# The feed-forward value product as three products of rounded high and low parts, with a new plan of phases

## The chip, the cores and the metric

The kernel runs on one core of a Trainium2 chip. The metric is the device time of one launch in microseconds (us). The times shown are medians over several runs of the same program; one further execution was profiled.

## The reference

The input is `x` of shape (8, 1024, 256) in 32-bit floats: 8 sequences of 1024 tokens with 256 channels. Three layers are added to it in turn.

```python
x = x + 0.5 * ffn(layernorm(x), W_r, W_k, W_v, mu_r, mu_k)
x = x + attention(layernorm(x), qkv_w, qkv_b, out_w, out_b, gate_w, gate_b, pos_bias, scale_embed, if_gain)
x = x + 0.5 * ffn(layernorm(x), W_r, W_k, W_v, mu_r, mu_k)

def ffn(x, W_r, W_k, W_v, mu_r, mu_k):
    x_prev = x shifted by one token, with zeros in front
    xr = mu_r * x + (1 - mu_r) * x_prev
    xk = mu_k * x + (1 - mu_k) * x_prev
    r = sigmoid(xr @ W_r.T)
    k = xk @ W_k.T
    return r * (square(relu(k)) @ W_v.T)
```

The attention has 16 heads of 16 channels. Each token looks at 40 fixed distances behind it (0 to 32, and 48, 64, 96, 128, 192, 256, 384), with a logit that is scaled by a learned vector for each distance, a softmax over the 40, and a sigmoid gate ahead of the output projection. All three weight matrices of the feed-forward layer are 256 x 256, and both feed-forward layers use the same ones. The change is in the last product, `square(relu(k)) @ W_v.T`.

## The kernel before

The 8192 tokens are cut into 32 chunks of 256. For each chunk the program has three generators: `ffn(c, "a")` (the first feed-forward layer), `project(c)` (the projections of the attention) and `ffn(c, "b")` (the second feed-forward layer). The attention has `far` and `local`, which compute scores by blocks and write them to HBM skewed, and `attend(tt)` for each tile of 128 tokens, which reads them back, adds the bias, takes the softmax and multiplies with the values.

Each `yield` ends a phase. The order of all work is written out by hand: the table `PLAN` gives every phase of a generator a place in units of chunks, `WARP` shifts the places of the first four and the last ten chunks, and at the end of `macaron` all phases are sorted by place and run in that order. So each engine has a fixed queue of instructions, served in order. A phase that is moved in `PLAN` moves its instructions on every engine and its transfers in the queues of SP and ACT.

One feed-forward layer on one chunk goes so:

- `normed` (L206 to L226): statistics on DVE, eight small instructions on POOL, the scaling on ACT (L224), and four transposes on PE (L226), which leave channels on partitions.
- the mixing with the token before: four instructions on ACT (L241), four on DVE (L246) into the tile `xm`; `xk` and `xr` are its halves.
- the key product with `wk`: four 32-bit products of 128 x 128 by 256 columns, then the relu on ACT (L263) back into `xk`.
- the gate product with `wr`, four more, and the square of `xk` on ACT (L269, in place), then the tanh (L271).
- the value product with `wv`, four more, with `xk` as the stationary side: `mm(p[:, i], xk[:, h, i * 128 : i * 128 + 128], wv[:, h], h == 0, h == 1)`.
- the gating on DVE (L278) and the addition to the token's row on POOL (L280).

The attention's projections in `project` are already made of high and low parts in 16-bit floats: `wa_hi`, `wa_lo` for the weights, `xh` and `xl` for the data, and three products (high by high, high by low, low by high) in place of each one. ACT rounds `xh` (L291), and DVE computes the rest `xl` (L292). In the profile a 32-bit product appears as two records, a 16-bit one as one.

PSUM has three banks for these products (`bank`, the tag `psf`). `xm`, and so `xk`, has one buffer for each of the two layers.

Of the kernel before, what the change touches and what calls it, by code (L numbers as in the profile page):

```python
# [7 lines left out]

F32 = mybir.dt.float32
F16 = mybir.dt.float16  # L10
I32 = mybir.dt.int32
AF = mybir.ActivationFunctionType
# [30 lines left out]


PLAN = {
    "setup": (94.301, 95.430, 96.861),
    "f1": (-6.891, -5.181, -4.113, -3.628, -3.556, -3.503, -3.223, -3.134, -3.030, -2.933, -2.814, -2.771),
    "p": (-2.636, -2.595, -2.382, -2.366, -2.209, -2.155, -2.084, -1.868, -1.644, -1.528, -1.432),
    "f2": (1.626, 1.748, 1.930, 2.004, 2.060, 2.208, 2.297, 2.414, 2.553, 2.580, 2.713, 4.437),
    "far": (  # L50
        (-0.987, -0.918),
        (-0.874, -0.608),
        (-0.990, -0.939),
        (-0.777, -0.772),
        (-0.751, -0.627),
        (-0.528, -0.523),
    ),
    "loc": (
        (-1.515, -1.348),
        (-0.848, -0.610),  # L60
        (-1.298, -1.048),
        (-1.496, -1.489),
    ),
    "att": (
        (-0.277, -0.025, -0.020, 0.011, 0.092, 0.296, 0.358, 0.413, 0.416, 0.471, 0.743, 0.779, 0.784, 0.838, 0.892, 0.971, 1.094, 13.222),
        (-0.404, 0.000, 0.016, 0.041, 0.111, 0.194, 0.295, 0.315, 0.427, 0.447, 0.621, 0.660, 0.673, 0.723, 0.824, 0.884, 0.938, 1.093),
    ),
}
WARP = {
    ("att", 0): 0.012, ("att", 1): 0.014, ("att", 2): 0.002, ("att", 3): -0.006, ("att", 22): 0.010, ("att", 23): 0.002, ("att", 24): -0.008, ("att", 25): 0.032, ("att", 26): 0.048, ("att", 27): 0.036, ("att", 28): 0.026, ("att", 29): -0.049, ("att", 30): -0.064, ("att", 31): -0.076,  # L70
    ("f1", 0): -1.203, ("f1", 1): -0.910, ("f1", 2): -0.739, ("f1", 3): 0.153, ("f1", 22): 0.006, ("f1", 23): 0.025, ("f1", 24): -0.009, ("f1", 25): -0.004, ("f1", 26): 0.009, ("f1", 27): 0.026, ("f1", 28): 0.017, ("f1", 29): 0.027, ("f1", 30): 0.045, ("f1", 31): 0.053,
    ("f2", 0): 0.006, ("f2", 1): 0.006, ("f2", 2): -0.013, ("f2", 3): 0.001, ("f2", 22): 0.006, ("f2", 23): -0.003, ("f2", 24): 0.043, ("f2", 25): 0.041, ("f2", 26): 0.025, ("f2", 27): 0.477, ("f2", 28): 0.422, ("f2", 29): 0.543, ("f2", 30): 0.373, ("f2", 31): 0.119,
    ("far", 0): -0.275, ("far", 2): -0.001, ("far", 22): 0.004, ("far", 24): 0.035, ("far", 26): 0.044, ("far", 28): 0.047, ("far", 30): -0.024,
    ("loc", 0): -0.699, ("loc", 1): -0.010, ("loc", 2): 0.023, ("loc", 3): 0.047, ("loc", 22): 0.037, ("loc", 23): 0.007, ("loc", 24): 0.043, ("loc", 25): 0.074, ("loc", 26): 0.045, ("loc", 27): 0.056, ("loc", 28): 0.007, ("loc", 29): 0.037, ("loc", 30): 0.014, ("loc", 31): 0.120,
    ("p", 0): -0.906, ("p", 1): -0.868, ("p", 2): -0.096, ("p", 3): 0.024, ("p", 22): -0.017, ("p", 23): -0.005, ("p", 24): 0.014, ("p", 25): 0.005, ("p", 26): -0.008, ("p", 27): -0.040, ("p", 28): 0.034, ("p", 29): 0.045, ("p", 30): 0.006, ("p", 31): -0.018,
}


# [5 lines left out]
def macaron(ctx: ExitStack, tc: tile.TileContext, x, wffn, watt, wo, cols, rows, pbias, se, mask, out):  # L84
    nc = tc.nc
# [3 lines left out]

    ident = const.tile([128, 128], F32, name="ident")  # L90
    make_identity(nc, ident)
    w_f = const.tile([128, 3, 2, 256], F32, name="w_f")
    wr, wk, wv = w_f[:, 0], w_f[:, 1], w_f[:, 2]
    col = const.tile([128, 14], F32, name="col")
    mu_r, mu_k, b_q, b_k, b_g, gain, slot = (col[:, 2 * i : 2 * i + 2] for i in range(7))
    wot = const.tile([128, 2, 256], F32, name="wot")
# [25 lines left out]
    pga = pool("pga", PGA)  # L122
    lazy = {}

    def setup():
        with tc.tile_pool(name="setup", bufs=1) as sp:
            nc.sync.dma_start(w_f, wffn.rearrange("w (c p) d -> p w c d", p=128))
            wst = sp.tile([128, 4, 2, 256], F32, name="wst")
            nc.sync.dma_start(wst, watt.rearrange("w (c p) d -> p w c d", p=128))
            nc.sync.dma_start(row, rows.unsqueeze(0).to_broadcast([128, 2, 256]))  # L130
            zero = sp.tile([128, 4 * 512], F32, name="zero")
            nc.gpsimd.memset(zero, 0.0)
            nc.sync.dma_start(bias[:, 3].rearrange("p u e -> p (u e)"), pbias.to_broadcast([128, NO * 16]))
            msk = sp.tile([128, 3, NO], F32, name="msk")
            nc.sync.dma_start(msk, mask.rearrange("t p u -> p t u"))
            nc.sync.dma_start(wot, wo.rearrange("(c p) d -> p c d", p=128))
            se_f = sp.tile([128, NO], F32, name="se_f")
            nc.sync.dma_start(se_f, se.unsqueeze(0).to_broadcast([8, 16, NO]))
            yield
            nc.gpsimd.tensor_scalar(w_f[:, 2], w_f[:, 2], 0.25, 0.0, ALU.mult, ALU.add)  # L140
            for t in vw:
                nc.gpsimd.memset(t, 0.0)
            for t in ks:
                nc.gpsimd.memset(t[:, 0:LW], 0.0)
            for i in range(2):
                nc.sync.dma_start(v_d[i][0 : VPAD * VROW].rearrange("(p w) -> p w", p=VPAD), zero[:VPAD, :VROW])
            for sf in sf_d:
                nc.sync.dma_start(sf[0:PADF].rearrange("(p w) -> p w", p=16), zero[:16, : PADF // 16])
                for c0, c1, w in ((0, 5, 384), (5, 10, 384), (10, 15, 384), (15, 16, 368)):
                    o = PADF + c0 * ROW + ROW - 384  # L150
                    nc.sync.dma_start(flat(sf, o, (SF_T, 32), (ROW, c1 - c0), (1, w)), zero[:32, : (c1 - c0) * w])
            nc.sync.dma_start(flat(pd_d, NL * 16, (4 * SKEW, 128), (SKEW, 4), (1, SKEW - NL * 16)), zero[:, : 4 * 512])
            nc.vector.tensor_scalar(wst[:, 0], wst[:, 0], 0.25 * WS, None, ALU.mult)
            nc.vector.tensor_scalar(wst[:, 1:4], wst[:, 1:4], WS, None, ALU.mult)
            nc.scalar.copy(wa_hi, wst)
            nc.vector.tensor_tensor(wa_lo, wst, wa_hi, ALU.subtract)
            nc.vector.tensor_scalar(b_q, b_q, 0.25 * WS, None, ALU.mult)
            nc.vector.tensor_scalar(b_k, b_k, WS, None, ALU.mult)
            nc.vector.tensor_scalar(bv, bv, WS, None, ALU.mult)
            nc.vector.tensor_scalar(b_g, b_g, 0.5, None, ALU.mult)  # L160
            yield
            for t in range(3):
                nc.gpsimd.tensor_tensor(
                    bias[:, t], bias[:, 3], msk[:, t].unsqueeze(2).to_broadcast([128, NO, 16]), ALU.add
                )
            for c in range(2):
                nc.vector.tensor_scalar(wot[:, c], wot[:, c], gain[:, c : c + 1], 0.5 / WS, ALU.mult, ALU.mult)
            nc.vector.tensor_scalar(se_f, se_f, 4.0 / WS, None, ALU.mult)

            nc.vector.tensor_reduce(  # L170
                own.rearrange("p (h q) -> p h q", h=2),
                ident.rearrange("p (q h d) -> p h q d", q=4, h=2),
                AX.X,
                ALU.add,
            )
            nc.vector.tensor_reduce(
                kown.rearrange("p (h q) -> p h q", h=2),
                own.rearrange("p (h r q) -> p h q r", h=2, r=2),
                AX.X,
                ALU.add,  # L180
            )
            nc.vector.tensor_tensor(
                seb.rearrange("p u h q -> p u (h q)"),
                se_f.unsqueeze(2).to_broadcast([128, NO, 4]),
                kown.unsqueeze(1).to_broadcast([128, NO, 4]),
                ALU.mult,
            )
        lazy["pat"] = pool("pat", 2)
        lazy["pv1"] = pool("pv1", 2)
        yield  # L190
# [3 lines left out]
    def mm(o, l, r, start, stop):  # L194
        nc.tensor.matmul(o, l, r, start=start, stop=stop)  # L195
# [34 lines left out]
    def ffn(c, s):  # L230
# [35 lines left out]
        for i in range(2):  # L266
            for h in range(2):
                mm(p[:, i], xr[:, h, i * 128 : i * 128 + 128], wr[:, h], h == 0, h == 1)
        nc.scalar.activation(xk, xk, AF.Square)  # L269
        yield  # L270
        nc.scalar.activation(xr, p, AF.Tanh, scale=0.5)  # L271
        yield
        p = bank([128, 2, 256], "p")
        for i in range(2):
            for h in range(2):
                mm(p[:, i], xk[:, h, i * 128 : i * 128 + 128], wv[:, h], h == 0, h == 1)
        yield
        nc.vector.scalar_tensor_tensor(xr, xr, 1.0, p, ALU.add, ALU.mult)  # L278
        yield
# [290 lines left out]
    add = lambda kind, place, gen, times: steps.extend(  # L570
        (move(kind, place) + t, kind, j, gen) for j, t in enumerate(times)
    )
    add("0", -100, setup(), PLAN["setup"])
    for c in range(NCH):
        add("f1", c, ffn(c, "a"), PLAN["f1"])
        add("p", c, project(c), PLAN["p"])
# [73 lines left out]
```

## Time and profile before

| | |
|---|---|
| median of 3 runs | 1022.88 us (1022.44 to 1028.41) |
| the profiled execution's own time | 1026.83 us |
| its span | 1024.8 us |
| PE busy | 951.4 us (93%) |
| PEld busy (weight loads, beside PE) | 781.3 us (76%) |
| DVE busy | 831.9 us (81%) |
| POOL busy | 695.5 us (68%) |
| ACT busy | 610.4 us (60%) |
| DMA | 208.75 MB, 204 GB/s |

PE is TensorE, DVE is VectorE, ACT is ScalarE, POOL is GpSimd, and SP is the engine that issues most transfers. A share of the span averages over a start, a long middle and an end. In the start and the end few chunks are under way, and the engines wait for each other; in the middle the phases of many chunks overlap. The span is the profiled execution's, on the one core.

### The profile page before, as it was taken

What the parts mean: (1) busy time and instruction counts of PE and PEld (TensorE: products, weight loads), DVE (VectorE), ACT (ScalarE), POOL (GpSimd) and SP (SyncE); (2) the same over time, 40 slices, a digit from 0 to 9 for tenths busy, and PEclk for the clock granted to TensorE, in tenths of its full rate; (3) what the DMA queues carried; (4) which work ended last, traced back from release to release, by engine and by line L of the source; (5) the groups of instructions that cost most, each with busy time, mean ns of one, the idle gap of its engine ahead of it and who ended that gap; (6) DMA issues with size and microseconds to landing.
All of it is one profiled execution on the core that took longest, in us unless ns stands there. A gap on an engine that the chain in (4) does not pass through costs nothing.

```text
span 1024.8 us, 36078 instructions
## 1 busy us (share of the span) xinstructions
PE 951.4 (93%) x14592; PEld 781.3 (76%) x14592; DVE 831.9 (81%) x1670; ACT 610.4 (60%) x1218; POOL 695.5 (68%) x1240
## 2 busy tenths in 40 slices
PE   3888899999999999999999999999999999976775
PEld 2666688888888888888888888888888888854554
DVE  4446889988999789888999789988999789866761
ACT  3454666676666766676666766676666766543332
POOL 5434778767877688667787678767886778543641
PEclk9899999999999999999999999999999999988888
DMA  8257777768777776777877777688776777757530
GB/s 241 62 157 204 221 227 200 222 200 249 214 219 216 215 237 198 214 228 218 236 207 225 220 237 211 196 236 244 222 212 210 205 227 216 211 161 234 166 110 21
DMA packets 204365, 208.75 MB, mean 204 GB/s; under 512 B 77288, under 2 KB 162472, under 8 KB 204200
## 3 DMA queue, kind: packets, MB, share of 16 engines
q1 hardware_dynamic: 194984, 189.16, 64.8%
q10 hardware_dynamic: 9216, 17.31, 4.6%
q8 instruction: 114, 1.87, 0.8%
q14 instruction: 51, 0.42, 0.1%
HBM read 110.26 MB, written 96.14 MB: 201 GB/s over the span
## 4 chain that ended last, share of the span: by engine, by line
PE 81%; DMA 4%; POOL 4%; DVE 4%; issue 3%; ACT 2%; SPq 1%; ACTq 0%; POOLq 0%; DVEq 0%
PE p L195 55%; PE pv L195 6%; PE tra L195 5%; PE tra L514 5%; PE tr L226 5%; PE gp L195 4%; PE tra L547 1%; DMA lg<-sl 1%; ACT xn L224 1%; POOL y L213 1%; POOL x L280 1%; DMA sf<-sf 1%; DVE prod L505 1%; DMA pd<-pd 1%; DVE st L207 1%
## 5 line engine op out<-in xcount | busy, mean ns | idle before, releaser
L195 PE MATMUL p<-w_f,xm 128*128 128x256 f32 x1024 | 251.3, 389 | 0.0
L195 PEld LDWEIGHTS p<-w_f,xm 128*128 128x128 f32 x1024 | 187.5, 192 | 42.2 <-issue 12.7
L461 POOL TENSOR_TENSOR lg<-lg,bias 128x640 f32<-128x640 f32 x64 | 99.0, 1547 | 85.8 <-DVE lg L458 74.6
L195 PE MATMUL p<-xm,w_f 128*128 128x256 f32 x512 | 128.6, 396 | 8.4 <-DVE xm L248 5.2
L224 ACT ACTIVATE xn<-x,nb,y 128x256 f32<-128x256 f32 x192 | 104.9, 599 | 32.4 <-POOL nb L219 16.4
L241 ACT ACTIVATE xm<-tr,col 128x256 f32<-128x256 f32 x256 | 100.4, 475 | 39.8 <-PE tr L226 33.9
L195 PE MATMUL p<-kst,qst 64*32 64x256 f32 (+1 forms) x4096 | 123.6, 362 | 0.5 <-DVE kst L317 0.3
L246 DVE SCALAR_TENSOR_TENSOR xm<-tr,rest,xm 128x255 f32<-128x255 f32 x256 | 105.5, 474 | 21.2 <-ACT xm L241 19.9
L195 PEld LDWEIGHTS p<-xm,w_f 128*128 128x128 f32 x512 | 96.5, 198 | 25.6 <-issue 10.4
L508 POOL TENSOR_TENSOR far<-prod 128x272 f32<-128x272 f32 x64 | 49.0, 765 | 93.3 <-DVE prod L505 86.2
L280 POOL TENSOR_TENSOR x<-x,xm 128x512 f32<-128x512 f32 x64 | 81.9, 1279 | 39.9 <-DVE xm L278 39.9
L195 PE MATMUL p<-xh,wa_hi 128*128 128x256 f16 x384 | 105.1, 274 | 0.0
L195 PE MATMUL p<-xh,wa_lo 128*128 128x256 f16 x384 | 104.9, 273 | 0.0
L195 PE MATMUL p<-xl,wa_hi 128*128 128x256 f16 x384 | 104.9, 273 | 0.0
L482 POOL TENSOR_TENSOR prod<-vn,lg 128x272 f32<-128x272 f32 x144 | 94.9, 671 | 14.2 <-ACT lg L467 12.8
L520 ACT COPY ptt<-tra 128x512 f32<-128x512 f32 x128 | 74.7, 584 | 43.7 <-PE tra L514 27.8
L226 PE MATMUL tr<-ident,xn 128*128 128x128 f32 x384 | 66.4, 293 | 33.2 <-ACT xn L224 32.7
L505 DVE TENSOR_TENSOR prod<-prod 128x544 f32<-128x544 f32 (+2 forms) x120 | 93.6, 780 | 3.6
L195 PEld LDWEIGHTS pv<-vw,ptt 128*32 128x32 f32 x4096 | 69.2, 157 | 33.3 <-ACT ptt L520 17.3
L195 PEld LDWEIGHTS p<-kst,qst 64*32 64x32 f32 x4096 | 75.7, 122 | 22.9 <-issue 10.7
L317 DVE SCALAR_TENSOR_TENSOR kst<-p,col,kown 128x1024 f32<-128x1024 f32 x64 | 78.7, 1271 | 13.5 <-PE p L195 13.5
L514 PE MATMUL tra<-ident,pd 128*128 128x128 f32 x512 | 80.1, 280 | 10.3 <-DMA pd<-pd 6.7
(79 smaller groups left out, 2051.5 us busy)
## 6 DMA issues: line engine op xcount, KB each, us to landing
sl<-sl SPq DMA_DIRECT2D x256, 128.0 KB, 3.4
pd<-pd SPq DMA_DIRECT2D x64, 512.0 KB, 4.3
sf<-sf SPq DMA_DIRECT2D x184, 128.0 KB, 3.2
vw<-vd SPq DMA_DIRECT2D x128, 136.0 KB, 4.1
v<-vd SPq DMA_DIRECT2D x64, 272.0 KB, 4.4
lg<-sl SPq DMA_DIRECT2D x64, 264.0 KB, 3.9
pd<-lg ACTq DMA_DIRECT2D x64, 264.0 KB, 2.8
vd<-vn SPq DMA_DIRECT2D x32, 272.0 KB, 4.8
```

What stands on the lines that cost most here:

```text
L195: nc.tensor.matmul(o, l, r, start=start, stop=stop)
L224: nc.scalar.activation(xn, x2[:, i], AF.Identity, bias=nb[:, i : i + 1], scale=y[:, i : i + 1])
L226: nc.tensor.transpose(tr[:, c, i * 128 : i * 128 + 128], xn[:, c * 128 : c * 128 + 128], ident)
L241: nc.scalar.activation(xm[:, o, h], tr[:, h], AF.Identity, scale=mu[:, h : h + 1])
L246: nc.vector.scalar_tensor_tensor(x_[:, 1:256], tr[:, h, 0:255], m, x_[:, 1:256], ALU.mult, ALU.add)
L280: nc.gpsimd.tensor_tensor(x2, x2, xr, ALU.add)
L317: nc.vector.scalar_tensor_tensor(ks[g][:, o : o + 256], p[:, g].unsqueeze(2).to_broadcast([128, 256, 4]), b_k[:, g : g + 1], kown.unsqueez ...
L461: nc.gpsimd.tensor_tensor(la, la, bias[:, min(t, 3)].rearrange("p u e -> p (u e)"), ALU.add)
L482: nc.gpsimd.tensor_tensor(prod[:, k], shifted[k][1](), lf[:, k].unsqueeze(2).to_broadcast([128, 16, 17]), ALU.mult,)
L505: nc.vector.tensor_tensor(terms[:, 0:m], terms[:, 0:m], terms[:, n - m : n], ALU.add)
L514: nc.tensor.transpose(tr[:, pr * 128 : pr * 128 + 128], pd.rearrange("p (m e) -> p m e", e=8)[:, :, 4 * g + pr], ident,)
L520: nc.scalar.copy(ptt.rearrange("p q n -> p (q n)"), tr)
```

## The change

The value product's weights get tiles of their own in the format `float32r` (a 32-bit word whose value is rounded to fewer bits): `wvh` holds the rounded weights, `wvl` what the rounding left off. `wv` itself is only needed in the setup. For each chunk and layer ACT computes the square twice, once rounded into the new tile `kh` and once in full into `xk`; POOL subtracts the two into the new tile `kl`, in a phase of its own. The four products of the value matrix become twelve. `kh` and `kl` have one buffer each, and both layers share them.

In the setup one transfer of the three weight matrices becomes two (`w_f` with `wr` and `wk`, then `wv`), ACT makes `wvh`, and POOL makes `wvl`. All numbers of `PLAN` and `WARP` are new; each feed-forward generator has one phase more.

```diff
+F32R = mybir.dt.float32r
...
-    "f1": (-6.891, -5.181, -4.113, -3.628, -3.556, -3.503, -3.223, -3.134, -3.030, -2.933, -2.814, -2.771),
+    "f1": (-7.302, -4.764, -4.509, -3.640, -3.589, -3.493, -3.268, -3.145, -3.058, -3.042, -2.949, -2.896, -2.784,),
...
-    "f2": (1.626, 1.748, 1.930, 2.004, 2.060, 2.208, 2.297, 2.414, 2.553, 2.580, 2.713, 4.437),
+    "f2": (1.617, 1.671, 1.900, 1.957, 2.027, 2.186, 2.230, 2.282, 2.339, 2.447, 2.552, 2.641, 4.246,),
...
-    w_f = const.tile([128, 3, 2, 256], F32, name="w_f")
-    wr, wk, wv = w_f[:, 0], w_f[:, 1], w_f[:, 2]
+    w_f = const.tile([128, 2, 2, 256], F32, name="w_f")
+    wr, wk = w_f[:, 0], w_f[:, 1]
+    wvh = const.tile([128, 2, 256], F32R, name="wvh")
+    wvl = const.tile([128, 2, 256], F32R, name="wvl")
...
-            nc.sync.dma_start(w_f, wffn.rearrange("w (c p) d -> p w c d", p=128))
+            wffn = wffn.rearrange("w (c p) d -> p w c d", p=128)
+            nc.sync.dma_start(w_f, wffn[:, 0:2])
+            wv = sp.tile([128, 2, 256], F32, name="wv")
+            nc.sync.dma_start(wv, wffn[:, 2])
...
-            nc.gpsimd.tensor_scalar(w_f[:, 2], w_f[:, 2], 0.25, 0.0, ALU.mult, ALU.add)
+            nc.gpsimd.tensor_scalar(wv, wv, 0.25, 0.0, ALU.mult, ALU.add)
+            nc.scalar.copy(wvh, wv)
+            nc.gpsimd.tensor_tensor(wvl, wv, wvh.bitcast(F32), ALU.subtract)
...
+        kh = pw.tile([128, 2, 256], F32R, name="kh")
+        nc.scalar.activation(kh, xk, AF.Square)
         nc.scalar.activation(xk, xk, AF.Square)
         yield
         nc.scalar.activation(xr, p, AF.Tanh, scale=0.5)
         yield
+        kl = pw.tile([128, 2, 256], F32R, name="kl")
+        nc.gpsimd.tensor_tensor(kl, xk, kh.bitcast(F32), ALU.subtract)
+        yield
         p = bank([128, 2, 256], "p")
         for i in range(2):
             for h in range(2):
-                mm(p[:, i], xk[:, h, i * 128 : i * 128 + 128], wv[:, h], h == 0, h == 1)
+                n = slice(i * 128, i * 128 + 128)
+                for q, (l, r) in enumerate(((kh, wvh), (kh, wvl), (kl, wvh))):
+                    mm(p[:, i], l[:, h, n], r[:, h], h == 0 and q == 0, h == 1 and q == 2)
         yield
         nc.vector.scalar_tensor_tensor(xr, xr, 1.0, p, ALU.add, ALU.mult)
```

In the middle of the run POOL's changed queue has the new subtraction behind the two additions to the rows of other chunks (L280, L341) in one layer, and behind the far products (L482) of an attention tile in the other. Behind it stand the eight small instructions of a norm in the one case, and the bias addition of an attention tile (L461) in the other. On PE other groups of products stand between a chunk's key product and its value product, as they did before.

## The prediction

> **What bounds the kernel now.** I read the page's engine table first, then busy time by windows, then what each engine waited for between 100 and 900 us, and last the chain that ended last.
>
> ```profile
> PE 951.4 (93%) x14592; PEld 781.3 (76%) x14592; DVE 831.9 (81%) x1670; ACT 610.4 (60%) x1218; POOL 695.5 (68%) x1240
> ...
> 100.00:900.00 800.00, 793.86 (x12664) 663.28 (x12671) 710.95 (x1420) 520.40 (x1046) 597.16 (x1046) 1.00 0.75 219
> ```
>
> The second line is the window from 100 to 900 us: length, then busy time of PE, PEld, DVE, ACT and POOL, the granted clock, the share of the DMA engines. PE is busy 793.86 of 800 us at full clock, so this middle is bound by PE, and less PE work there is less time. DVE is next with 89%, POOL has 75%, ACT 65%. The start and the end are not PE's: of PE's 1024.8 - 951.4 = 73.4 idle us, 67 lie before 100 and after 900.
>
> How much room POOL and DVE have is seen in what they waited for in the same window (total us, times, longest):
>
> ```profile
> POOL lg L461 <- DVE lg L458: 62.3, 36, 4.8
> POOL far L508 <- DVE prod L505: 61.6, 29, 3.2
> POOL va L212 <- DVE mv L208: 15.0, 22, 5.9
> POOL prod L482 <- ACT lg L467: 8.3, 10, 3.0
> ```
>
> With two smaller rows (2.8 and 0.2) POOL waited 150.2 us; the other 649.8 us are its own, with the small gaps between its instructions. The same sum for DVE is 73 us of waiting.
>
> The chain shows what one group of products costs while PE runs without a break:
>
> ```profile
> 493.16 1.73 PE p L195 x8
> 494.89 0.44 PE tra L514 x4
> 495.33 1.31 PE p L195 x12
> 496.65 0.44 PE tra L514 x4
> ```
>
> Start, length, line, records. The x8 is a group of four 32-bit products (two records each), 0.2165 us a record; the x12 is a group of twelve 16-bit products, 0.109 us each; the x4 are four transposes of 128 columns with 32-bit operands, one record and 0.11 us each. These spacings, and not the "mean ns" of the groups, which overlap, are the price on PE.
>
> One chunk of the middle takes 28.8 us: the same piece of the chain (3.04 us, x20) stands at 207.38 and at 668.00, sixteen chunks later. So 800 us hold 27.8 chunks, 55.6 of the 64 value products.
>
> **The change, part by part.** *The value product.* It loses 8 records of 0.2165, 1.73 us, and gains 12 products of the rounded format, which the trace does not show. From below, the 16-bit row: 0.109 each, 1.31 us, a gain of 0.42. From above, the 32-bit record of the same 256 columns: 0.2165 each, 2.60 us, a loss of 0.87. Break-even is 1.73 / 12 = 0.144. The transposes lean to the upper end, since one record with 4-byte operands takes 0.11 us for 128 columns. But they and the 32-bit records must carry the full word, and the rounded format, like the 16-bit one, need not: one record, a rounded value. I take 0.109 and keep 0.2165 for the range. Gain in the middle: 55.6 x 0.42 = 23.3 us. Of the 8.4 others, where PE is busy some 70%, I count half: 1.7 us.
>
> *Weight loads.* Twelve come where eight were. The 16-bit loads have this row, and their products still follow at 0.109 us:
>
> ```profile
> L195 PEld LDWEIGHTS <-wa_hi 128*128 128x128 f16 x768 | 74.5, 98 | 13.3 <-issue 3.1 <-DVE st L207 0.8
> L514 PEld LDWEIGHTS tra<-ident,pd 128*128 128x128 f32 x512 | 71.2, 190 | 18.9 <-DVE lg L465 4.9 <-ACT ptt L520 3.4 <-issue 2.9
> ```
>
> So a load of 98 ns lies beside the product ahead of it, and a 32-bit load with its transpose keeps to 0.11 us a pair. I cost the loads at nothing; if that cover went, 0.098 us more for each would make the group 2.48 us, the slow end again.
>
> [...]
>
> *ACT.* One more square per layer and chunk, at the row of the old one:
>
> ```profile
> L269 ACT ACTIVATE xm<-xm 128x512 f32<-128x512 f32 x64 | 40.8, 638 | 4.9 <-DMA sf<-sf 4.8
> L280 POOL TENSOR_TENSOR x<-x,xm 128x512 f32<-128x512 f32 x64 | 81.9, 1279 | 39.9 <-DVE xm L278 39.9
> L341 POOL TENSOR_TENSOR x<-x,row 128x512 f32<-128x512 f32 x32 | 56.2, 1755 | 1.1 <-ACT xn L224 1.1
> ```
>
> Two a chunk are 1.28 us, and ACT goes from 65% to about 72% of a shorter chunk: hidden behind PE. Behind it wait the square in place, the tanh and the copies L520, each 0.64 us later.
>
> *POOL.* One subtraction of the shape of L280: 1.28 us, with L341's 1.76 as the upper bound (that row reads a broadcast operand, this one does not) and no lower one below L280 for the same two operands. Two a chunk with gaps of 0.08 are 2.7 us. POOL's own work in a chunk is 649.8 / 27.8 = 23.4 us; it becomes 26.1 in a chunk of 28.8 - 0.84 = 27.96. It fits, with 1.9 us to spare in place of 5.4; by L341's price 0.9. DVE's spare falls from 2.6 to 1.8 us. So three engines are above 90%, and a late transfer is absorbed less often. PE's idle in the middle is 6.1 us; I add 3.
>
> *The new wait.* The third product waits for `kl`. After the key product come, by rows, the relu 0.60, a copy L520 0.59, two squares 1.28, the subtraction 1.28 and some 0.5 of hand-over: 4.3 us. In the changed queue the groups that stand between the end of the key product and the value product come to 6.45 us in one layer and 8.55 in the other at the spacings above. So 2 us are left for POOL's queue, where far, L280, the memset and L341 stand ahead of the subtraction in one layer. Hidden; without cover every microsecond too late costs one on PE, and then the gating L278, L280 and the next norm. Where a chunk is alone nothing covers it. Before, the last chunk's wr and wv followed its wk without a break, from 999.83 to 1005.13. Now relu, both squares and the subtraction end about 1005.1 and ten products follow: 1006.3, 1.2 us more. The same at the start: 2.4 together.
>
> *Setup and plan.* One transfer more on SP, a scaling POOL had before, one ACT copy (0.6) and one subtraction (1.3), all before the first value product, behind which DMA and norms wait longer: nothing counted; 1.9 if uncovered. The plan moves each phase on every queue, SP's transfers with it: loads of `x` come 0.41 chunk (12 us) earlier, stores of the result 0.19 chunk (5 us) earlier, and stores of `v` and scores change places with loads of `pd` and `lg`. No count changes but that one. Between the square's phase and the value product lie 0.196 chunk now against 0.193 before, so the longer chain was not paid for by distance. I cost the order at 0, with -7 to +10 us: a tenth of the idle 67 us won, or one more lost wait like the longest at 406 us (7.0) with a short one.
>
> **The sum**, on the profiled execution's own time: 1026.83 - 23.3 - 1.7 + 3 + 2.4 = 1007.2. That execution is 3.95 us above the median of the runs, and I carry this over: 1003.
>
> **Rivals.** *POOL and DVE give part of it back.* For: POOL's waits follow DVE's order and need not shrink on demand. If 2.3 of the 5.4 us of waiting a chunk remain in place of 1.9, a chunk is 26.1 + 2.3 = 28.4, and 0.44 x 27.8 = 12 us are added to the forecast: half the gain, 1015. Against: the waits are many and short, as of an engine that is early. *POOL becomes the bound, slower.* Place: the subtraction in POOL's queue ahead of L461 and the norms; point: more than 2.7 us of waiting left in a chunk (26.1 + 2.7 = 28.8). With 3.5 left, 27.8 x 0.8 = 22 us more: 1045. Against: 26.1 is below 27.96. *The rounded product streams like a 32-bit record, slower.* 55.6 x 0.87 + 3.6 at the ends + 5.4 = 57 us more: 1080; from 0.144 us a product it is no gain. For: the transposes. *The plan wins more*: the full 27 us and 3 at the ends: 993. *The change does nothing*: excluded, since the queue holds the twelve products.
>
> **How the numbers follow.** Forecast 0.68, half the gain 0.12, POOL's bound 0.05, slow products 0.10, a better plan 0.05. The likeliest case's own range is 996 to 1011; the range for 8 in 10 goes from 993 over the half gain and the upper cost of the order to 1024. About 1% (10 us) is what a measurement of this kernel can tell from no change. Below 1012.7 lie the forecast, the better plan and a part of the half gain: 0.74. Within 1%: 0.12. Slower by more: 0.14.
>
> **What would show it.** Right: groups of twelve rounded products of 1.31 us in the chain, PE still above 98% in the middle, a chunk of about 27.9 us, POOL about 86% busy there (24.04 of 27.96 us a chunk), and its waits near a third of what they were. Wrong: 2.6 us for a group; a PE that waits for `kl` (L284) in the middle; or idle time at the ends that moves by more than 10 us.

## The result and the profile after

The changed kernel is slower: 1085.15 us, median of 3 runs (1084.27 to 1088.4), against 1022.88 before. The ratio is 1.0604, with a 95% interval of 1.0555 to 1.0654. The forecast was 1003, and 1085 lies outside its range. The profiled execution took 1084.27 us, with a span of 1082.5.

The engine row of the page and the window from 100 to 900 us (length; busy time of PE, PEld, DVE, ACT and POOL; granted clock; share of the DMA engines; GB/s) answer to the first two lines that the prediction showed:

```profile
PE 956.3 (88%) x14848; PEld 784.1 (72%) x14848; DVE 853.0 (79%) x1670; ACT 651.4 (60%) x1283; POOL 775.7 (72%) x1305
...
PE 46%; DMA 15%; POOL 13%; DVE 8%; ACT 7%; issue 7%; SPq 3%; ACTq 0%; POOLq 0%; DVEq 0%
```

```profile
100.00:900.00 800.00, 763.47 (x12286) 635.95 (x12286) 693.91 (x1363) 531.50 (x1053) 634.28 (x1060) 0.99 0.73 209
```

PE is no longer the bound of the middle: it is idle for 36.5 of these 800 us, where it was idle for 6.1. No other engine has taken its place, since DVE (87%), POOL (79%) and ACT (66%) all stand below 90%. The second row is the chain that ended last: PE holds 46% of it, DMA 15%, POOL 13%. The same row of the kernel before:

```profile
PE 81%; DMA 4%; POOL 4%; DVE 4%; issue 3%; ACT 2%; SPq 1%; ACTq 0%; POOLq 0%; DVEq 0%
```

A chain that jumps between engines like the later one is one of waits, not of work.

The changed kernel has longer code, so its line numbers are larger: all products stand at L203 (before: L195), the two squares at L278 and L279, the subtraction at L284, the addition of the output bias to the row at L356 (L341), the loads of `vw`, `v3` and `pd` at L450, L456 and L512 (L435, L441, L497), the products on POOL at L497 (L482), the transposes of `pd` at L529 (L514) and the copy `ptt` at L535 (L520). The kernels of the experiments have one of the two sets, or one that is off by a few lines.

What PE waited for between 200 and 900 us (total us, times, longest): all rows of the kernel before, then the four largest of the changed kernel, then the two waits of SP's queue that grew (before, the same two came to 9.2 and 1.7 us):

```profile
PE pv L195 <- ACT ptt L520: 2.1, 2, 1.1
PE p L195 <- issue: 0.2, 1, 0.2
```

```profile
PE tra L529 <- DMA pd<-pd: 13.2, 10, 2.3
PE pv L203 <- ACT ptt L535: 5.2, 9, 1.0
PE tr L234 <- ACT xn L232: 5.2, 12, 0.5
PE p L203 <- POOL kl L284: 1.7, 2, 0.9
```

```profile
SPq L450 <- PE tr L234: 62.8, 29, 4.8
...
SPq L456 <- POOL prod L497: 42.9, 18, 4.3
```

SP's waiting is not in itself a loss: before, SP stood 152.5 us at the load of `pd`, for the store of the same data (after: 54.1), and PE paid nothing for it.

The wait that the prediction feared, for `kl`, is nearly absent. The largest is for the transfer `pd`, which the change does not touch in the code. The chain shows how it comes to be late (start, us, what):

```profile
511.08 0.06 ACT kh L278
511.14 0.09 POOL vn L355
511.23 1.74 POOL x L356
512.97 1.24 POOL kl L284
...
514.57 0.71 POOL y L221
...
516.50 0.85 POOL nb L226
...
517.62 1.83 POOL prod L497 x3
...
519.47 0.36 SPq L456
...
520.44 5.98 DMA pd<-pd
...
526.55 0.68 PE tra L529 x4
```

Read it from the bottom. The transposes on PE wait for the load of `pd` (L512). SP issues that load behind the load of `v3` (L456), and the load of `v3` waits until POOL's products L497 have released a buffer. Those products stand behind the norm, and the norm behind the subtraction `kl`. So POOL's 1.24 us are paid two queues further on. The transfer itself took 5.98 us here, where its median is 4.9 (4.3 before). The order on SP is the new plan's: the even tile's load of `pd` (phase 0.516) stands behind the odd tile's loads of `vw` and `v3` (0.484), where before it stood ahead of them (0.471 and 0.500).

The gap on PE then costs more than its own length. Three windows from the same place:

```profile
523.00:527.00 4.00, 1.75 (x16) 1.40 (x15) 3.32 (x6) 1.44 (x3) 3.83 (x4) 1.00 0.92 297
527.00:530.40 3.40, 3.40 (x19) 2.66 (x18) 1.60 (x3) 1.22 (x2) 2.83 (x9) 0.52 0.94 274
530.40:533.00 2.60, 2.60 (x54) 2.11 (x56) 2.60 (x3) 2.28 (x5) 2.60 (x5) 0.98 0.37 37
```

PE was idle for 2.25 us ahead of 526.55, and for the next 3.4 us the granted clock is 0.52: twelve 16-bit products take 2.56 us (the chain above goes on with `PE p L203 x12`), where they took 1.31. The four transposes behind them take 0.85 us in place of 0.44. So this gap cost about 2.25 + (2.56 - 1.31) + (0.85 - 0.44) = 3.9 us.

The span can be cut into three parts by the DVE sums `far<-pv` (L536 before, L551 after), one for each tile of 128 tokens: up to the start of the 7th, from there to the 55th (24 chunks), and behind. All values are us of the profiled execution, the middle one for each chunk:

| kernel | start | a chunk | end |
|---|---|---|---|
| before | 185.3 | 28.78 | 148.7 |
| after | 203.1 | 29.94 | 160.8 |
| e2, new plan alone | 195.6 | 29.46 | 162.6 |
| e3, after without the subtraction | 197.5 | 29.56 | 157.3 |
| e5, after, three `v3` buffers | 195.2 | 29.43 | 162.5 |
| e1, old plan, new arithmetic | 204.9 | 32.26 | 151.6 |
| e9, the same, `kl` earlier | 194.6 | 29.93 | 150.8 |
| e11, old plan, products alone | 188.0 | 28.32 | 143.1 |
| e12, before, second square | 187.1 | 29.01 | 147.9 |
| e13, before, subtraction | 187.9 | 29.19 | 145.7 |

Of the 57.7 us by which the span grew, 17.8 lie at the start, 24 x 1.16 = 27.8 in the middle and 12.1 at the end.

### The profile page after: what moved, and what is told of

It reads as the page before. It is cut to its first block, busy times and chain, and to the rows that moved or that the text cites. A ratio compares the mean times of both kernels' runs of the same rounds, so it can differ in the third digit from the quotient of the medians.

```text
span 1082.5 us, 36811 instructions
## 1 busy us (share of the span) xinstructions
PE 956.3 (88%) x14848; PEld 784.1 (72%) x14848; DVE 853.0 (79%) x1670; ACT 651.4 (60%) x1283; POOL 775.7 (72%) x1305
## 4 chain that ended last, share of the span: by engine, by line
PE 46%; DMA 15%; POOL 13%; DVE 8%; ACT 7%; issue 7%; SPq 3%; ACTq 0%; POOLq 0%; DVEq 0%
PE p L203 30%; DMA pd<-pd 6%; DMA lg<-sl 4%; PE pv L203 3%; PE tra L203 3%; PE tra L529 3%; PE tr L234 3%; POOL prod L497 3%; PE gp L203 3%; ACT xn L232 2%; POOL kl L284 2%; DMA lg<-sf 2%; POOL y L221 2%; DVE st L215 1%; ACT ptt L535 1%
## 5 line engine op out<-in xcount | busy, mean ns | idle before, releaser
L203 PE MATMUL p<-xm,w_f 128*128 128x256 f32 x512 | 135.2, 411 | 12.2 <-DVE xm L256 6.6
L203 PE MATMUL p<-kst,qst 64*32 64x256 f32 (+1 forms) x4096 | 125.4, 362 | 2.6 <-issue 2.1
L284 POOL TENSOR_TENSOR kl<-xm,kh 128x512 fp32r<-128x512 f32 x64 | 89.5, 1398 | 50.5 <-ACT xm L279 41.0
L203 PE MATMUL p<-w_f,xm 128*128 128x256 f32 x512 | 124.7, 387 | 0.0
L203 PEld LDWEIGHTS p<-xm,w_f 128*128 128x128 f32 x512 | 99.4, 205 | 33.5 <-issue 9.5
L535 ACT COPY ptt<-tra 128x512 f32<-128x512 f32 x128 | 74.7, 584 | 68.4 <-PE tra L529 35.7
L234 PE MATMUL tr<-ident,xn 128*128 128x128 f32 x384 | 70.7, 299 | 43.2 <-ACT xn L232 41.8
L203 PE MATMUL p<-xl,wa_hi 128*128 128x256 f16 x384 | 106.7, 278 | 1.0 <-DVE xl L307 1.0
L203 PE MATMUL p<-xh,wa_hi 128*128 128x256 f16 x384 | 106.9, 278 | 0.7 <-ACT xh L306 0.7
L529 PE MATMUL tra<-ident,pd 128*128 128x128 f32 x512 | 82.4, 285 | 28.1 <-DMA pd<-pd 21.1
L203 PE MATMUL p<-xh,wa_lo 128*128 128x256 f16 x384 | 106.8, 278 | 0.0
L497 POOL TENSOR_TENSOR prod<-vn,lg 128x272 f32<-128x272 f32 x144 | 100.1, 707 | 8.6 <-ACT lg L482 6.9
L203 PEld LDWEIGHTS p<-w_f,xm 128*128 128x128 f32 x512 | 96.1, 197 | 12.4 <-ACT xm L271 0.5
L529 PEld LDWEIGHTS tra<-ident,pd 128*128 128x128 f32 x512 | 72.9, 192 | 40.3 <-issue 21.4
L520 DVE TENSOR_TENSOR prod<-prod 128x544 f32<-128x544 f32 (+2 forms) x120 | 97.4, 811 | 4.4 <-POOL prod L497 0.8
L385 ACT ACTIVATE sl<-p 128x512 f32<-128x512 f32 x128 | 72.9, 645 | 41.6 <-PE p L203 40.4
```

The source lines that it names most:

```text
L234: nc.tensor.transpose(tr[:, c, i * 128 : i * 128 + 128], xn[:, c * 128 : c * 128 + 128], ident)
L284: nc.gpsimd.tensor_tensor(kl, xk, kh.bitcast(F32), ALU.subtract)
L497: nc.gpsimd.tensor_tensor(prod[:, k], shifted[k][1](), lf[:, k].unsqueeze(2).to_broadcast([128, 16, 17]), ALU.mult,)
L520: nc.vector.tensor_tensor(terms[:, 0:m], terms[:, 0:m], terms[:, n - m : n], ALU.add)
L529: nc.tensor.transpose(tr[:, pr * 128 : pr * 128 + 128], pd.rearrange("p (m e) -> p m e", e=8)[:, :, 4 * g + pr], ident,)
L535: nc.scalar.copy(ptt.rearrange("p q n -> p (q n)"), tr)
```

## The experiments

### Plan or arithmetic: e1 and e2

e1 is the changed kernel with the plan of before; the added phase, with the subtraction, takes the tanh's old place and the tanh stands just behind the square. e2 is the kernel before with the new plan.

```diff
 e1: PLAN and WARP of before, and
-    "f1": (... -3.223, -3.134, -3.030, -2.933, ...)
+    "f1": (... -3.223, -3.134, -3.110, -3.030, -2.933, ...)
-    "f2": (... 2.208, 2.297, 2.414, ...)
+    "f2": (... 2.208, 2.297, 2.330, 2.414, ...)
 e2: PLAN and WARP of after, without the phase of kl (-3.042 and 2.339)
```

> The three rounded products and the subtraction, in the phases of the kernel before; the subtraction's new phase lies halfway between the tanh and the value product. Theory A (the subtraction loads POOL's queue, and what stands behind it comes late: the norms, the release of buffers, and through SP's queue the loads of pd): still slow, 1050 to 1100 us. Theory B (the new plan of phases loses the time, the products gain): 1000 to 1015 us. Theory C (PE waits for kl itself): 1050 or more, with over 20 us of PE waiting for L284 in the middle.

> The new plan of phases with the four 32-bit products as before, without the second square and the subtraction. Theory A: 1025 to 1045 us, since the queue of POOL is as light as before, with PE doing 0.30 us more a group than the changed kernel. Theory B: 1070 us or more. Theory C: about 1025 to 1045 as well.

Measured: e1 1130.68 us, ratio 1.1014 (1.0978 to 1.1049); e2 1063.79 us, ratio 1.0361 (1.0305 to 1.0417); the kernel before, measured beside them, took 1025.83. Both parts are slower by themselves. Of the whole loss the new plan alone makes 38 us, and on the old plan the new arithmetic costs 105. So the new plan suits the new arithmetic better than the old one does, but is a bad order in itself. In e1 the wait for `kl` is real (PE, 200 to 900 us):

```profile
PE p L203 <- POOL kl L284: 42.7, 28, 3.1
```

### What of the arithmetic costs, on the new plan: e3 and e4

```diff
 e3:
-        kl = pw.tile([128, 2, 256], F32R, name="kl")
-        nc.gpsimd.tensor_tensor(kl, xk, kh.bitcast(F32), ALU.subtract)
 e3, e4:
-                for q, (l, r) in enumerate(((kh, wvh), (kh, wvl), (kl, wvh))):
+                for q, (l, r) in enumerate(((kh, wvh), (kh, wvl), (kh, wvh))):
```

> The changed kernel without the subtraction: the third product reads kh in place of kl, so the low part of the square is left out of the result while PE's work stays the same. Theory A: 1010 to 1035 us, with SP's waits for POOL's L497 near the 2 us of the kernel before. Theory B: above 1060. Theory C: 1010 to 1035.

> The changed kernel with the subtraction on POOL as it is, but its result is read by nobody: the third product reads kh, so the low part of the square is left out of the result. This parts POOL's load from the wait for kl. Theory A: within 1.5% of the changed kernel, 1070 to 1090 us. Theory C: like the run without the subtraction, 1010 to 1035. Theory B: above 1060.

Measured: e3 1064.97 us, ratio 1.0379 (1.0345 to 1.0414); e4 1083.5 us, ratio 1.0555 (1.0522 to 1.0588). With both squares and the new products, but no subtraction, the time is that of the plan alone (1063.79); every theory but the one of the plan had it 30 us lower. With the subtraction executed and read by nobody it is 18.5 us more, nearly the 1085 of the whole change. So on the new plan the price of the subtraction is the time that it takes in POOL's queue, not PE's wait for its result.

### The queue behind the subtraction: e10 and e5

```diff
 e10: att, even tile
-        (..., 0.444, 0.451, 0.516, 0.695, ...)
+        (..., 0.444, 0.451, 0.480, 0.695, ...)
 e5:
-        lazy["pv1"] = pool("pv1", 2)
+        lazy["pv1"] = pool("pv1", 3)
```

> The changed kernel with one number of the plan changed: the load of pd of the even tile is moved from 0.516 to 0.480 chunks, so that it stands in SP's queue ahead of the loads of vw and v3 of the odd tile instead of behind them. Theory A2 (in the middle the time is lost where SP waits for POOL's L497 to free the v3 buffer, with the pd load that PE's transposes need queued behind it; each late load also lowers the clock for some us): PE's waits for pd fall from 13 us in 200 to 900 us to below 4, a chunk takes 28.8 to 29.4 us in place of 30.1, the time is 1045 to 1065. Rival (POOL is simply full, and the late norms and sums show elsewhere): 1075 to 1090.

> The changed kernel with three v3 buffers in place of two, so that SP's load of v3 does not wait for POOL's L497. Theory A2: SP's waits for L497 vanish (43 us in 200 to 900 us now), though SP still waits for vw ahead of it (63 us); some of the loss goes, 1055 to 1075. Rival (POOL is full): 1075 to 1090.

Measured: e10 1088.95 us, ratio 1.0632 (1.0573 to 1.0691), no gain; e5 1067.76 us, ratio 1.0425 (1.0391 to 1.0458). Taking the `pd` load out of the queue behind `v3` removes PE's wait for `pd`, and its idle time returns under other names: `ptt` 10.3, `xn` 9.2 and `kl` 7.3 us. A third buffer for `v3`, so that SP need not wait for POOL's products, gains 17 us, about the price of the subtraction in e4, and PE's two largest waits become

```profile
PE p L203 <- POOL kl L284: 10.5, 11, 1.7
PE tr L234 <- ACT xn L232: 4.0, 8, 0.8
```

So in the kernel as changed, the wait for the `v3` buffer that the chain showed costs about as much as the subtraction does. That the one is the other's price is not shown: the third buffer was not tried without the subtraction, where SP still waits 32.9 us for those products (e3) and 29.5 (e2). And e10 shows that the order of the two loads alone is not worth anything, since the next waits stand ready.

### The arithmetic by parts, on the old plan: e11, e12, e13, e8, e9

```diff
 e11: before's plan; nc.scalar.activation(kh, xk, AF.Square) in place of the square,
      twelve rounded products, the third of each three reads kh (low part left out)
 e12: before, and a second nc.scalar.activation(kh, xk, AF.Square), unused
 e13: before, and nc.gpsimd.tensor_tensor(kl, xk, x2, ALU.subtract) in the tanh's phase, unused
 e8:  e1 without the subtraction, third product reads kh
 e9:  before's plan, kl's phase ahead of the tanh (-3.115 and 2.345), the tanh where it was
```

> The kernel before, with its own phases untouched, and only the products changed: twelve rounded ones in place of four, with one square on ACT (straight into kh) and nothing on POOL; the low part of the square is left out of the result. If the products' own term was right (0.30 us a group by the trace of the changed kernel, and PE bounds the middle): 1000 to 1010 us. If PE does not turn its 0.30 us into time: 1020 or more.

> The kernel before with one more square on ACT ahead of the old one, into a tile that nobody reads. By the prediction ACT has room and this costs nothing: 1020 to 1027. By the theory that ACT's order holds PE up (the copies for pv and the scalings for the next transposes stand behind the squares): 1030 to 1050.

> The kernel before with a subtraction on POOL in the phase of the tanh, of the size of kl, which waits for the square and which nobody reads. POOL's load alone, in the old order: by the prediction it is hidden, 1020 to 1030; by the theory that POOL's queue is too tight, 1040 to 1090, through late norms, sums and buffers.

> The phases of the kernel before with the three rounded products, and no subtraction: the third product reads kh, so the low part of the square is left out of the result. What the products gain when POOL and the order are as before: with 0.30 us a group, 64 x 0.30 = 19 us less if PE stays the bound, 1003 to 1012. If the longer way over ACT (two squares) or the order holds PE up by itself: 1020 or more.

> The phases of the kernel before with the three rounded products, and the subtraction ahead of the tanh and earlier in POOL's queue: at -3.115 in place of -3.030 in the first layer, 2.345 in place of 2.414 in the second, so that neither the far products nor a norm stand between the square and the subtraction. If the loss of the run with the old phases was the wait for kl behind other work in POOL's queue (43 us of it in 200 to 900, and the clock): 1010 to 1045. If POOL's load itself is the loss: 1090 or more.

Measured:

| run | us | ratio (95%) |
|---|---|---|
| e11, products alone | 1012.36 | 0.9866 (0.9811 to 0.9922) |
| e12, second square alone | 1033.66 | 1.0084 (1.0057 to 1.0112) |
| e13, subtraction alone | 1036.7 | 1.0125 (1.0092 to 1.0158) |
| e8, products and second square | 1039.5 | 1.0143 (1.0103 to 1.0183) |
| e9, all three, `kl` early | 1063.07 | 1.0386 (1.0351 to 1.042) |

The products alone are a gain, of 11 us. In e11's middle window PE has 788.34 of 800 us:

```profile
100.00:900.00 800.00, 788.34 (x13084) 664.68 (x13082) 722.38 (x1437) 523.25 (x1050) 600.22 (x1053) 1.00 0.76 221
```

The second square costs 10 us in the kernel before and 27 beside the new products (e8 against e11). The subtraction costs 13 us in the kernel before, 24 with everything else (e9 against e8), and 91 where it stands one phase later (e1 against e8). In e8 and e1 the tanh stands a little earlier than in e11 and e9, and a part of these differences may come from that. On the old plan the parts together cost more than the sum of what they cost singly. That each uses up the same little room between two queues would explain it; no run shows this by itself.

How the time is lost on PE can be read from start to start of its groups, in the 24 chunks of the table above. In e12 the transposes of `xn` take 1.68 us a chunk (1.58 before) and the products `pv` behind the copy `ptt` 2.36 (2.25): most of the 0.23 us by which a chunk grew. In e13 the transposes of `xn` take 1.70 and those of `pd` 1.95 (1.80): 0.27 of the 0.41 us by which a chunk grew there. So PE does wait a little longer behind ACT and POOL, in many small pieces.

There is a second way by which the subtraction can cost time on the old plan. In e13 DVE is busy for 862.2 us and in e9 for 883.8, with the same 1670 instructions that took 831.9 before; the last section shows sums on DVE that took 1.98 us in place of 1.00 beside an addition on POOL. No run parts this from the delay in POOL's queue. On the new plan it is small: 846.2 us without the subtraction (e3), 851.7 with it (e4).

In e9 PE's wait for `kl` falls from 42.7 to 12.2 us, but now POOL stands still until the square is there, with all that is queued behind it (POOL, 200 to 900 us):

```profile
POOL kl L282 <- ACT xm L279: 39.9, 26, 4.3
```

Early, the subtraction blocks POOL; late, it blocks PE.

### A version from these: e14

e9's order with the value product of `f1` a little later (-2.905), the subtraction of `f2` at 2.360 in place of 2.345, three `v3` buffers, and the row of L341 expanded beforehand instead of broadcast.

> An attempt to mend the change: the kernel before's phases, the three products, the subtraction ahead of the tanh (at -3.115, and at 2.360 behind L356 in the second layer), the first layer's value product 0.028 chunk later, three v3 buffers, and the output bias spread to both tiles of a chunk in the setup so that L356 reads it without a broadcast. If late subtractions and the v3 wait were what remained: 1010 to 1035. If ACT's second square and DVE's load set the rest: 1040 to 1060.

Measured: 1061.42 us, ratio 1.0351 (1.0318 to 1.0385), within 2 us of e9. With the expanded row POOL's addition took 1.69 us on average, with the broadcast 1.40 in e9 and 1.76 in the kernel before; so the broadcast, to which the prediction had put its 1.76, was not its cost. No version of the whole change that was run beats the kernel before.

### What in the new plan costs: e15, e16, e18, e22

```diff
 e15: e2 with the WARP of before
 e16: e2 with the even tile's pd load at 0.480
 e18: both
 e22: e16, and in "p"
-    ... -2.252, -2.201, -2.149, ...
+    ... -2.252, -2.153, -2.149, ...
```

> The kernel before with the new plan of phases, but the old table WARP (which shifts the phases of the first and the last chunks alone); no rounded products, one square, no subtraction. With both new tables the kernel before took 1063.8 us, 40.6 us of span more: 10.3 before the seventh far-from-pv sum, 16.4 over the 48 chunks' worth of middle, 13.9 behind. Theory A (the ends are set by WARP, the middle by the phases): the 24 us of the ends come back and the middle keeps its 16: 1036 to 1044. Rival B (the phases set the ends too): 1058 or more. If only one end answers: 1049 to 1055.

> The kernel before with both new tables, and the even tile's load of pd moved from phase 0.516 to 0.480, so that it stands in SP's queue ahead of the odd tile's loads of vw and v (0.484), as it does before the change. Theory A (that load, held behind two loads which wait for PE and POOL, is what costs the middle its 16 us): about 1046 to 1050, and PE's waits for pd nearly gone. Rival B (the buffers of vw and v are released too late for the new phases, so SP's waiting only moves to the next reader): 1060 to 1066, PE's idle time then named by ptt, xn or the scores.

> The kernel before with the new phases, the old WARP and the even tile's pd load at 0.480. If WARP makes the loss at the ends and the order of the loads that in the middle: 1021 to 1030, no slower than before by more than a few us, and the new plan's loss is explained. If the loads' order only moves the waiting: 1036 to 1044, the same as with the old WARP alone. If the phases set both: 1058 or more.

> The kernel before with both new tables, the even tile's pd load at 0.480, and the key projection's twelve products (step 5 of the list p) back between the even tile's second group of transposes and its value products: -2.201 becomes -2.153. In the kernel before they stand there; in the new plan they stand ahead of the transposes, and once pd comes in time PE waits up to 2.2 us for the copy ptt, which stands on ACT behind an exponential and the store of pd. Theory A (these two swaps are the middle's 16 us): 28.9 to 29.1 us a chunk in place of 29.45 and 1048 to 1054. Rival B (the waiting moves on once more): 29.3 or more and 1058 to 1066.

Measured: e15 1084.58 us, ratio 1.0576 (1.0524 to 1.0628); e16 1062.5 us, 1.0389 (1.0355 to 1.0424); e18 1079.63 us, 1.0545 (1.0509 to 1.0581); e22 1075.53 us, 1.0486 (1.0445 to 1.0526). With the old WARP and the new phases some steps of the first or last chunks come in another order than their data, so that part of the numbers differs in e15 and e18 (and in e17); the amount of work is the same.

The new WARP alone is not the cause: with the old one the new phases take 21 us more. Since the order in e15 is partly wrong, and both tables were made together, this does not show that WARP has no part in it. Nor is it one place in the middle. In e2 PE waits for `pd`; in e16 no longer, but a chunk still takes 29.45 us, and PE waits for the copy `ptt`. The timelines of ACT and of PE in e16 at such a place (start, us, engine, line, what, and in brackets the idle time before):

```profile
330.60 0.74 ACT L467 ACTIVATE lg<-lg 128x640 f32<-128x640 f32 x1
334.12 0.33 ACTq L468 DMA_DIRECT2D pd<-lg  x1
334.49 0.58 ACT L520 COPY ptt<-tra 128x512 f32<-128x512 f32 x1 [3.15 <-DMA lg<-sl]
```

```profile
330.71 0.60 PE L514 MATMUL tra<-ident,pd 128*128 128x128 f32 x4
331.15 1.89 PE L195 MATMUL p<-w_f,xm 128*128 128x256 f32 x8
335.12 0.27 PE L195 MATMUL pv<-vw,ptt 128*32 128x34 f32 x4 [2.08 <-ACT ptt L520]
```

The copy stands on ACT behind an exponential and the issue of a store, which comes 2.8 us after the exponential has ended. Between the transposes and the value products PE has one group of 1.89 us to do. Before the change the key projection's twelve products (`p`, sixth step) stood in this gap too. In e22 they are back in it, and this wait is gone (2.3 us in all), but now nothing lies between the two groups of transposes, and the second waits for the first one's copy:

```profile
PE tra L514 <- ACT ptt L520: 14.4, 15, 1.0
```

A chunk takes 29.82 us, more than without the move. Before the change one projection's products stood in each of the two gaps; the new plan has put one of the two ahead of both. e22 moved one of them and not both, which the expectation had overlooked; moving both was not tried.

### The same mends with the whole change: e17 and e23

e17 is the changed kernel with the old WARP and three `v3` buffers; e23 has three `v3` buffers and both moves of e22.

> The changed kernel with the old WARP and three buffers in place of two for the tile v (pool pv1); all of its arithmetic. Three buffers alone brought 1085 to 1068. Theory A (the two losses add up: WARP 20 to 24 us at the ends, the buffers 17 us): 1044 to 1050, still slower than before. Rival B (with the second square and the subtraction in the queues the ends do not answer to WARP): 1062 to 1068.

> The whole changed kernel with the same two moves in its plan and three buffers for the tile v. Three buffers alone gave 1068. Theory A (the two moves bring what they bring the kernel before, and the second square and the subtraction keep their price): 1052 to 1060. Rival B (ACT's and POOL's longer queues give the waiting another place): 1064 to 1072.

Measured: e17 1082.34 us, ratio 1.0578 (1.0548 to 1.0609); e23 1097.5 us, ratio 1.0697 (1.0661 to 1.0734). Both are worse than the three buffers alone (1067.76). As in the kernel before, each move opens another wait.

## Why the prediction was wrong, point by point

**The value product: right in direction, twice too large in size.** The rounded products stream like the 16-bit ones, with one record each. A group on PE (start, us, what):

```profile
515.61 0.28 PE L203 MATMUL p<-wvl,kh 128*128 128x256 f32 x1
515.73 0.29 PE L203 MATMUL p<-wvh,kl 128*128 128x256 f32 x1
515.86 0.28 PE L203 MATMUL p<-wvh,kh 128*128 128x256 f32 x1
515.97 0.28 PE L203 MATMUL p<-wvl,kh 128*128 128x256 f32 x1
```

They start 0.119 us apart, not 0.109, and the first of a group takes some 0.1 more. Counted from start to start over the 24 chunks of the middle, a group takes 1.54 us in e11, where the four 32-bit products took 1.83 (1.73, and here too 0.1 for the first): 0.29 each in place of the predicted 0.42. So 0.58 us a chunk are freed, of which e11 shows 28.78 - 28.32 = 0.46 as time; the rest is new waiting of PE. Over the whole run the 25.0 us of the prediction's two terms are 11 in e11.

The weight loads are hidden, as counted: in the profile of the changed kernel each of these loads takes 192 ns, and still the products start 0.119 us apart. The slow-product rival fell with them. I had chosen 0.109 by the argument that the 32-bit records carry the full word and the rounded ones need not; what makes the former take 0.2165 us no run shows.

**The second square and the subtraction as hidden work: wrong, and this is the first step that failed.** For both together the sum had 3 us of idle time on PE. I had sized the work well. ACT's square took 0.64 us, the subtraction 1.40 on average (1.28 forecast), and POOL's own time in the middle rose from 23.4 to (800 - 112.4) / 26.7 chunks = 25.7 us a chunk, where I had 26.1. What failed is the step from "the engine has room" to "the work is hidden". Alone they cost 10 and 13 us in a kernel where ACT is at 65% and POOL at 75%, and on the new plan the subtraction costs 18.5 (e4 against e3). In the traces an engine serves its queue in order (in the chain above POOL's products L497 began at 517.62, behind the 1.24 us of `kl` and the norm), so 0.64 us ahead of the copies `xn` and `ptt`, or 1.3 us ahead of the norm and the products L497, can delay these by that much; whether PE notices then depends on how soon the next reader comes, not on the share of the engine. The longer groups of `xn`, `ptt` and `pd` on PE fit this. For e13 and e9 the lengthened DVE instructions are the other reading, and the two were not parted. My rival of a POOL that becomes the bound had the right engine and the wrong rule: POOL was never full, and waited 112.4 us in the middle of after, where I had foreseen near a third of 150.

**The wait for `kl`: right on the new plan, not on the old.** It is 1.7 us in 700. On the old plan it is 42.7 us (e1) or 12.2 (e9), so it depends on where the subtraction stands in POOL's queue. How much of the cover on the new plan is the 6.45 and 8.55 us of PE's work that I had counted was not tested; when other waits go, 10.5 us (e5) and 7.3 us (e10) of this one come up. My comparison of distances also had a slip. In the first layer the square's phase and the value product stood 0.201 chunk apart before, not 0.193, against 0.196 now; in the second, which I left out, 0.256 against 0.217. So the longer chain got less distance, not more.

**The order at 0, with -7 to +10 us: wrong, the largest error.** The new plan alone costs 38 us (e2), of which 16.4 are in the middle and 24.2 at the ends by the parts of the span. I had named the swap of the loads of `v` with those of `pd`, and given it no price. What should have been asked is which read comes behind each transfer, and what lies between. Between 200 and 900 us of the kernel before PE never waited for `pd`, and that gives no hint that a plan with the same work would keep it so.

**The ends at 2.4 us: wrong.** They grew by 29.9, of which the plan alone makes 24.2. The old WARP does not bring them back (e15). In e2's chain the splitting of the weights, `wa_hi` and `wa_lo`, stands between 16.41 and 20.63 us ahead of the first chunk's gating on DVE, and in the chain of before it does not; this was only read, not tried, and no cause of the 24 us is shown.

**The account.** Measured beside each other: before 1025.83, the plan alone +38.0 (e2), the products and the second square on it +1.2 (e3), the subtraction's time on POOL +18.5 (e4). The whole change, measured at another time, is 1.7 us above e4. The products' gain is in the second term: it is worth 11 us by itself on the old plan. That the second square uses it up on the new one follows if it is worth as much there, which was not measured apart.

**What stays open.** Why the new phases cost 24 us at the ends, and whether any order lets the whole arithmetic run in less than the kernel before. In the middle the waits of the plan are named, but no single move took them away. For eight of the eighteen runs (e2, e9, e11, e13, e14, e17, e22, e23) the time lay in none of the ranges stated ahead of it: the picture of queues did not foretell these times.

## What to carry to other kernels

Here engines that were busy for 65 and 75% could not take 0.64 and 1.3 us more for nothing; their queues run in order. So ask what stands behind the new instruction, who reads it, and how much work the bound engine has between; price it by that margin, not by the share. A new order of the same work is a change of its own, to be costed wait by wait; here it was 38 of 62 us. And when a wait is removed and the time stays, look for the next wait in the same chain before you believe that the first was harmless.

## What the runs showed of the hardware

After a gap of 2.25 us on PE the granted clock was 0.52 for 3.4 us, by the windows above. The length of a gap alone did not decide it. In e4 PE waited 2.93 us for `pd`, up to 876.41, and the clock behind it stayed at 1.00:

```profile
873.40:876.40 3.00, 0.07 (x1) 0.02 (x1) 2.14 (x3) 0.84 (x2) 2.88 (x3) 1.00 0.93 343
876.40:880.00 3.60, 3.59 (x25) 3.25 (x26) 3.12 (x4) 1.85 (x3) 3.06 (x8) 1.00 0.91 290
```

Other gaps of these traces say the same. In the changed kernel gaps of 2.65, 2.15, 1.90 and 0.97 us on PE, up to 164.52, 286.86, 646.23 and 381.65, were followed, 0.3 to 2.1 us later, by 3.41 us at a clock of 0.50; gaps of 1.97 and 1.96 us, up to 766.51 and 886.22, were followed by full clock, and so was one of 2.36 us, up to 110.12, in the kernel before. What decides between the two the runs do not show.

In e13 some of DVE's sums took twice their time beside an instruction of POOL, 1.98 us in place of 1.00. There the subtraction shifts POOL's queue, so that its addition of the bias (L463 there) falls beside DVE's sum of 128 x 816 (L507; two instructions in the second line):

```profile
308.89 1.54 POOL L463 TENSOR_TENSOR lg<-lg,bias 128x640 f32<-128x640 f32 x1
```

```profile
309.27 2.86 DVE L507 TENSOR_TENSOR prod<-prod 128x816 f32<-128x816 f32 x2
```

The first of DVE's two took 2.03 us, from 309.27 to 311.30, where it takes 1.00 alone: it ends 0.87 us after POOL's has ended, and POOL's is not lengthened. In e13 19 of 48 such sums begin beside the addition of the bias, and take 1.98 us on average; each ends 0.86 to 0.87 us after it. In the kernel before only one begins early enough beside it to be lengthened, to 1.23 us; in e9 17 do. The line's group over the whole run, before and in e13 (busy us, mean ns):

```profile
L505 DVE TENSOR_TENSOR prod<-prod 128x816 f32<-128x816 f32 x48 | 48.2, 1004 | 0.0
```

```profile
L507 DVE TENSOR_TENSOR prod<-prod 128x816 f32<-128x816 f32 x48 | 67.0, 1395 | 0.0
```

So 19 of the 30 us that DVE is busy longer in e13 come from an instruction that the change does not touch. Why such a sum ends 0.86 to 0.87 us after POOL's addition no run shows. In the changed kernel on its new plan no such sum is lengthened by the addition of the bias. One began 0.16 us ahead of that addition and took 1.00 us; there POOL's addition took 2.23 us in place of some 1.55.
